# Attention and a quantised convolution block: band statistics behind both halves, and the last block's tail, the count and the scale factors at other places

## The chip, the cores and the metric

The kernel runs on one core of a Trainium2 chip. The metric is the device time of one execution in microseconds (us); the time of a kernel is the median of several runs. A profiled execution gives the trace, in which PE is TensorE's matmul, PEld its weight load, DVE VectorE, ACT ScalarE, POOL GpSimd and SP SyncE, which here only issues DMAs.

## The reference

Two layers on x of 4 x 128 x 64 x 64 in fp32. Cut to what is computed:

```python
# layer 0: group norm, attention with 4 heads of 32 channels over 4096 positions, projection, residual
x_norm = _group_norm(x, norm_w, norm_b)                    # 8 groups
qkv = einsum('oc,bchw->bohw', qkv_w, x_norm) + qkv_b
attn = softmax(einsum('bhid,bhjd->bhij', q, k) * scale)
out = einsum('bhij,bhjd->bhid', attn, v)                   # back to b, c, h, w
x = x + einsum('oc,bchw->bohw', proj_w, out) + proj_b
# layer 1: two 3x3 convolutions with weights quantised to 3 bits, each with batch norm
residual = x
out = relu(batchnorm(conv3x3(x, lsq_quantize(w1, alpha1)), gamma1, beta1))
out = batchnorm(conv3x3(out, lsq_quantize(w2, alpha2)), gamma2, beta2)
return relu(out + residual)
```

## The kernel before

Every engine works through its instructions in the order in which the program issues them; the order is written out by hand, and waits come from the tiles: whoever reads a tile waits for its writer, whoever writes it again waits for its readers. Tiles come from pools with a fixed number of buffers, so a new tile can wait for an old one's last reader. In PSUM there are three buffers of two banks (`pss`, for scores and for convolution sums) and two of one bank (`psa`). In SBUF a ring of nine buffers (`stack_tile`, one free buffer after the other in the order of their release) holds the attention's keys and, later, the bands and their parts.

*Attention.* 32 blocks (4 images, 8 query blocks each), 32 steps of key rows to a block. PE makes scores in groups of three half steps (L442), ACT takes exponentials (L444), PE weighs the values with them (L456) into `acc`, DVE adds the exponentials up (L471), and a few are added by DMA (`rm`, L466). `schedule` hangs other work on the half steps of a block; `ends` are the half steps that close a group of three. There the next image's norm is made: `late[b]` is the list of its steps, of which number 5 (L281, L282: two products for the biases of k and q, tile `gb`) and 6 (L286, their subtraction) stand at the first such slot of one block for each of three images, 7 and 8 (`gw`, `bvn`) at the third.

*The end of a block* is a chain (`finish_parts`): copy `acc` to `av` (ACT), `merge` the two sums (a DMA that adds, `r<-rm`, POOL's queue), `sums` over rows on PE (L488, tile `l`), `spread` the 2048 totals over partitions by DMA (`lq<-ls`), `invert` them on DVE and write them out (`rd<-rq`), adding totals and reciprocals to `worst`; `gather` them with copies by DMA (`rc<-rd`), `weigh` (`av` times `rc`, DVE L520), `project` (PE, tile `po`), `store` (DVE L530 adds bias and residual `x`, POOL's queue writes `y`). For all blocks but the last this chain is hung on the next block. For the last it is woven into the first convolution.

*Convolutions.* The image is cut into 16 bands of 16 rows, each of two halves of 512 positions. A band is loaded (`load_band`, SP's queue; POOL sets its borders, L543 to L549) and split into a high and a low part for exact products. A plain band (0, 1, 5, 8, 11, 15) takes 36 products, 18 to a half (`conv`, L811). The other ten are done two rows at a time (`conv_by_two`, L843) with 24 products: DVE makes sums and differences of rows (`begin`: L578 to L581, ACT copies them, L583), then the low parts (`rest`, L587); from the products the band's rows are put together by `copy` (ACT L853), `inner` (DVE L856, L857) and `outer` (L860, L862), and ACT sums squares (L948). For a plain band DVE takes statistics (`stats`, L904) and ACT copies the sums out (`keep`, L909). `stats` and `keep` read one half each of a tile that holds both; `origin` makes the shift of the squares from band 0's statistics. The split of band m+2 is made while band m's products run, and band m+3 is loaded.

`layer` runs this for a convolution; `first` says what the first one does beside each band. `opening` is the order of its bands 0 and 1, with the last block's chain up to `weigh`; `project` and `store` follow at band 3. At band 5 `count_bad` looks whether any total was out of range: a maximum over `worst` and a comparison on DVE, a product `nbad` of one number on PE in a buffer of `psa`, and a cast to `cnt` (L986 to L991), which every engine reads at the end to choose whether a general version is to run. Also at band 5 the second layer's quantised weights are loaded from `wqd` to `raw_w`, a buffer of the ring, and at band 6 DVE casts them to their own tile. Ahead of the first convolution DVE makes six scale factors of one column each for the batch norms (L870 to L872). `batch_norm` ends each layer.

The second convolution works in the same way (`second`); then the residual, loaded again from `y`, is added, and the output written.

Of the kernel before, what the change touches and what calls it, by code (L numbers as in the profile page):

```python
# [22 lines left out]
P = 128  # L23
# [55 lines left out]
def _fast_body(ctx, tc, x, norm_w, norm_b, qkv_wt, qkv_b, proj_wt, proj_b,  # L79
# [584 lines left out]
    def schedule(n, before):  # L664
        b, qb = blocks[n]
        todo = []
        ends = [p for p in range(2 * NK - 2) if (2 * n * NK + p) % 3 == 2]
        two = b + 1 < B and qb in ((3, 4, 5) if b == 0 else (2, 3))

        def at_half(p, f):  # L670
            todo.append((p, f))

        def add(kt, f):
            todo.append((2 * kt + 1, f))

        def visit(i, first, second, evacuate=None, split=True):
            at_half(ends[i], first)
            e = ends[i + 1 if split else i]  # L680
            at_half(e, second)
            if evacuate:
                at_half(e + 1, evacuate)
            return e

        if before:
            add(1, before["merge"])
            e = visit(5 if two or n == 1 else 6, lambda: before["sums"](0), lambda: before["sums"](1),
                      split=not two and n != 1)
            at_half(e + 2, before["spread"])  # L690
            at_half(e + 8, before["invert"])
            at_half(e + 12, before["residual"])
            at_half(e + 15, before["gather"])
            at_half(ends[18] - 4, before["weigh"])
            at_half(ends[18], before["project"])
            at_half(ends[18] + 2, before["store"])
        if n + 1 < len(blocks):
            add(22 if n == 0 else 14, lambda: load_q(*blocks[n + 1]))
        if n == 0:
            for i, what, j in ((0, "k", 5), (2, "v", 4), (4, "k", 6), (6, "v", 5), (8, "k", 7),  # L700
                               (10, "q", 1), (12, "v", 6), (14, "v", 7)):
                visit(i, *first_chunk(j, what, False), split=False)
                if what == "k":
                    at_half(ends[i] + 5, lambda j=j: load_k(0, j))
        if n == 0:
            for j in (2, 3):
                add(25 + j, lambda j=j: fetch(0, j))
        if n == 1:
            for i, j in zip((1, 3, 8, 10, 12, 14), range(2, NB)):
                if j > 3:  # L710
                    at_half(ends[i - 5], lambda j=j: fetch(0, j))
                visit(i, *project_parts(0, j, lambda j=j: xin[0, j])["q"], split=False)
        qn = qb if b else qb - 1
        if b + 1 < B:
            if qn == 1:
                st = small.tile([P, NB, 6], F32, name=f"st{b + 1}", tag="st")
                for j in range(NB):
                    add(3 * j // 2, lambda j=j: fetch(b + 1, j))
                    add(3 * j // 2 + 3, lambda j=j: nc.vector.bn_stats(st[:, j, :], xin[b + 1, j]))
                late[b] = norm_parts(b + 1, st)  # L720
                add(15, late[b][0])
                for i in (0, 1):
                    at_half(ends[13 + 2 * i], late[b][1 + 2 * i])
                    at_half(ends[13 + 2 * i] + 3, late[b][2 + 2 * i])
            if qn == 2:
                at_half(ends[0], late[b][5])
                at_half(ends[0] + 1, late[b][6])
                at_half(ends[2], late[b][7])
                at_half(ends[2] + 1, late[b][8])
            if b == 0:  # L730
                chunks = {2: (), 3: (0, 1), 4: (2, 3), 5: (4, 5), 6: (6,), 7: (7,)}
            else:
                chunks = {1: (), 2: (0, 1), 3: (2, 3), 4: (4,), 5: (5,), 6: (6,), 7: (7,)}
            for i, j in enumerate(chunks.get(qb, ())):
                p = project_parts(b + 1, j, lambda j=j: xin[b + 1, j])
                if not two:
                    for what, i in dict(k=1, q=10, v=13).items():
                        visit(i, *p[what])
                    continue
                for what, e in (dict(k=3, q=7, v=9) if i == 0 else dict(k=11, q=13, v=15)).items():  # L740
                    visit(e, *p[what], split=False)
                if i == 1:
                    add(8, lambda j=j: fetch(b + 1, j))
            if qn > 0 and qb + 1 in chunks:
                add(22, lambda j=chunks[qb + 1][0]: fetch(b + 1, j))
            if qb == NB - 1:
                for j in range(NB - 1):
                    add(4 * j + 1, lambda j=j: load_kv(b + 1, j))
        if b > 0 and qb == 0:
            add(9, lambda: load_k(b, NB - 1))  # L750
            add(16, lambda: load_v(b, NB - 1))


        if b == B - 1 and qb < NB - 1:
            for kt in (3, 11, 21):
                add(kt, lambda: next(pieces, None))
        elif 0 < b and qb == 0:
            for kt in (3, 12, 17, 22, 26) + ((29,) if b == 1 else ()):
                add(kt, lambda: next(pieces))
        if n == len(blocks) - 1:  # L760
            add(5, lambda: load_band(0, 0))
            add(13, lambda: split_band(0, 0))
            add(17, lambda: load_band(0, 1))
            add(24, lambda: split_band(0, 1))
            add(27, lambda: load_band(0, 2))
        return sorted(todo, key=lambda t: t[0])
# [80 lines left out]
    def rows_of_two(a, c, y, sums):  # L847
# [11 lines left out]
        def outer():  # L859
# [6 lines left out]

    a_q, a_g, a_n = ([small.tile([P, 1], F32, name=f"{n}{i}") for i in range(2)]
                     for n in ("aq", "ag_", "an"))
    for i in range(2):
        nc.vector.tensor_tensor(a_q[i], alpha_s[i], alpha_s[i], ALU.mult)  # L870
        nc.vector.tensor_tensor(a_g[i], alpha_s[i], bn[i][0], ALU.mult)
        nc.vector.tensor_scalar(a_n[i], a_g[i], -1.0, None, ALU.mult)  # L872

    def batch_norm(i, st):

# [121 lines left out]

    def first(m):
        begin = rest = nothing
        if 2 < m < len(bandlist) - 2:  # L1000
            begin, rest = parts_of(0, m + 2, raw[bandlist[m + 2]])

        def later():
            if m == 3:
                last = parts[len(blocks) - 1]
                last["project"]()
                last["store"]()
                att.close()
                pools["low"] = ctx.enter_context(tc.tile_pool(name="low", bufs=1, reuse_waits="tile"))
                cv.extend(pools["low"].tile([P, N], F32, name=f"cv{b}") for b in (2, 3))  # L1010
            if m == 5:
                count_bad()
                raw["w"] = f32(stack_tile("raw_w"))[:, : TAPS * P].rearrange("p (t o) -> p t o", o=P)
                nc.sync.dma_start(out=raw["w"], in_=wqd)
            if m == 6:
                nc.vector.tensor_copy(wq[1], raw["w"])
            if 2 < m < len(bandlist) - 3:
                load_band(*bandlist[m + 3])

        return begin, rest, later  # L1020

    def opening(banks, stats, keep, origin):
        last = parts[len(blocks) - 1]
        last["merge"]()
        e = [conv_tile(0, *bandlist[m]) for m in range(2)]
        conv(ready[0, 0, 0], e[0][:, 0, :], 0, wq[0])
        begin, rest = parts_of(0, 2, raw[bandlist[2]])
        begin()
        load_band(*bandlist[3])
        stats(0, 0, e[0])  # L1030
        keep(0, 0, e[0])
        conv(ready[0, 0, 0], e[0][:, 1, :], 1, wq[0])
        mix_weights(0)
        rest()
        last["residual"]()
        stats(0, 1, e[0])
        keep(0, 1, e[0])
        origin()
        conv(ready[0, 0, 1], e[1][:, 0, :], 0, wq[0])
        last["sums"](0)  # L1040
        last["sums"](1)
        last["spread"]()
        begin, rest = parts_of(0, 3, raw[bandlist[3]])
        begin()
        load_band(*bandlist[4])
        conv(ready[0, 0, 1], e[1][:, 1, :], 1, wq[0])
        stats(1, 0, e[1])
        keep(1, 0, e[1])
        last["invert"]()
        last["gather"]()  # L1050
        rest()
        stats(1, 1, e[1])
        keep(1, 1, e[1])
        done = banks(2)
        conv_by_two(ready[0, 0, 2], *done, 0)
        begin, rest = parts_of(0, 4, raw[bandlist[4]])
        begin()
        last["weigh"]()
        rest()
        load_band(*bandlist[5])  # L1060
        return {0: None, 1: None, 2: done}
# [532 lines left out]
```

## Time and profile before

| what | value |
|---|---|
| time, median of 3 runs | 2502.31 us (2500.63 to 2504.02) |
| profiled execution | 2501.34 us, its span 2499.6 us |
| PE busy | 2452.0 us (98%) |
| DVE busy | 2205.0 us (88%) |
| ACT busy | 2150.3 us (86%) |
| POOL busy | 282.3 us (11%) |
| first product of the first convolution | at 2230.46 us |
| first product of the second convolution | at 2359.34 us |
| end of the last product's line, c_last | DVE reads it at 2469.33 us |

The span runs from the first to the last instruction; the execution's time has 1.7 us around it. The attention takes the first 2230 us, the two convolutions some 240, the end some 30. An engine's busy share over the whole span says little about a stage of 60 us, so for the change the timeline of each engine from 2230 to 2360 us is read. In a timeline a line has its start, its length, the engine, the line of the program, the operation, what it writes and from what, how many instructions are merged, and in brackets how long the engine sat idle before it and who ended that. In a list of waits the numbers are the total, how often, and the longest.

### The profile page before, as it was taken

The page shows a single profiled execution, that of the slowest core. Times are in us where ns is not written, and L with a number is a line of the kernel's source. Part 1 is how long each engine was busy: PE and PEld are TensorE (multiplying, and loading weights), DVE is VectorE, ACT ScalarE, POOL GpSimd, SP SyncE. Part 2 cuts the span into 40 slices and gives each one's busy share as a digit, 9 for nine tenths or more (in the row PEclk, how much of TensorE's full clock was granted, in tenths as well). Part 3 has the DMA queues.
Part 4 walks back from the last instruction along what each step waited for, and adds up shares of the span by engine and source line. Part 5 has one row for each costly group of instructions (what it writes and reads, how often), then busy time and mean ns, then how long its engine had stood idle before and what let it go on. Part 6 is the DMA issues. An engine that isn't in the chain of part 4 may idle for free. (4 is left out here: it accounts for less than half of the span.)

```text
span 2499.6 us, 64813 instructions
## 1 busy us (share of the span) xinstructions
PE 2452.0 (98%) x28468; PEld 1463.4 (59%) x28468; DVE 2205.0 (88%) x1554; ACT 2150.3 (86%) x2347; POOL 282.3 (11%) x464
## 2 busy tenths in 40 slices
PE   9999999999999999999999999999999999999995
PEld 6555555555555555555555555555555555556774
DVE  6899888899988888889988898889999999997787
ACT  5999888999988899999988899999999999964475
POOL 2111111111011111110011111110000000110000
PEclk9999999999999999999999999999999999999998
DMA  6877677688766766788767766788656656665205
GB/s 197 191 183 171 165 176 176 167 202 193 180 154 164 182 163 164 161 204 193 163 149 184 168 157 168 172 203 188 146 130 152 143 132 149 152 139 111 86 1 203
DMA packets 149506, 405.17 MB, mean 162 GB/s; under 512 B 59712, under 2 KB 60480, under 8 KB 120544
## 3 DMA queue, kind: packets, MB, share of 16 engines
q0 software_dynamic: 45984, 281.44, 49.2%
q1 hardware_dynamic: 101360, 113.87, 17.4%
q8 instruction: 225, 3.69, 0.6%
q10 hardware_dynamic: 1872, 5.64, 0.6%
q14 instruction: 65, 0.53, 0.1%
HBM read 107.75 MB, written 56.43 MB: 66 GB/s over the span
## 5 line engine op out<-in xcount | busy, mean ns | idle before, releaser
L444 ACT ACTIVATE p<-s 128x1024 f32<-128x1024 f32 x2048 | 1951.3, 1033 | 197.9 <-PE s L442 152.6
L471 DVE TENSOR_TENSOR r<-r,p 128x2048 f32<-128x2048 f32 x768 | 1758.1, 2289 | 63.9 <-ACT p L444 13.2
L442 PE MATMUL s<-q,k 64*128 64x512 f32 x8192 | 1137.3, 409 | 1.2 <-ACT p L444 1.2
L456 PE MATMUL acc<-p,v 128*32 128x256 f32 x16384 | 1025.9, 383 | 0.0
L442 PEld LDWEIGHTS s<-q,k 64*128 64x128 f32 x8192 | 717.1, 185 | 406.3 <-issue 163.5
L456 PEld LDWEIGHTS acc<-p,v 128*32 128x32 f32 x16384 | 464.0, 109 | 481.8 <-issue 247.8
L466 POOL DMA_DIRECT2D rm<-p x160 | 139.1, 870 | 796.7 <-ACT p L444 618.3
L352 DVE SCALAR_TENSOR_TENSOR kst<-pk,b,kst 128x512 fp32r<-128x512 f32 x32 | 24.0, 751 | 82.7 <-PE s L442 62.3
L469 DVE TENSOR_TENSOR r<-p,p 128x2048 f32<-128x2048 f32 x32 | 73.2, 2288 | 11.7 <-ACT p L444 11.6
L948 ACT ACTIVATE uo<-cv,shift 128x1024 fp32r<-128x1024 f32 x20 | 23.1, 1153 | 61.0 <-DVE cv L862 57.3
L352 DVE SCALAR_TENSOR_TENSOR qst<-pq,b,qst 128x512 fp32r<-128x512 f32 x32 | 24.0, 750 | 58.2 <-PE s L442 47.3
L356 POOL DMA_DIRECT2D qd<-qst x31 | 23.6, 760 | 266.4 <-DVE qst L352 222.8
L811 PE MATMUL c<-hi,wq 128*128 128x512 f32 x180 | 48.4, 415 | 5.3 <-ACT cv L909 4.0
L492 POOL DMA_DIRECT2D r<-rm x32 | 27.0, 844 | 225.5 <-DMA rm<-p 93.8
L811 PE MATMUL c<-lo,wq 128*128 128x512 f32 x180 | 46.6, 404 | 0.0
L811 PEld LDWEIGHTS c<-hi,wq 128*128 128x128 f32 x180 | 34.8, 195 | 15.6 <-ACT cv L909 4.5
L356 POOL DMA_DIRECT2D kd<-kst x27 | 20.0, 741 | 175.7 <-DVE kst L352 167.2
L811 PEld LDWEIGHTS c<-lo,wq 128*128 128x128 f32 x180 | 34.4, 191 | 9.2
L317 PE MATMUL po<-av,wp 128*32 128x512 f32 x256 | 33.4, 593 | 4.6 <-DVE cv L860 3.2
L488 PE MATMUL l<-r,ones 128*32 128x256 f32 x512 | 37.7, 379 | 0.0
L464 POOL DMA_DIRECT2D rm<-p x32 | 17.9, 558 | 174.1 <-DMA r<-rm 82.3
L351 ACT ACTIVATE kst<-pk,b 128x512 fp32r<-128x512 f32 x32 | 22.3, 700 | 17.7 <-PE pk L317 17.6
(252 smaller groups left out, 1142.9 us busy)
## 6 DMA issues: line engine op xcount, KB each, us to landing
rm<-p POOLq DMA_DIRECT2D x192, 1024.0 KB, 7.9
r<-rm POOLq DMA_DIRECT2D x32, 1024.0 KB, 7.6
q<-qd SPq DMA_DIRECT2D x248, 128.0 KB
x<-in_x_dram SPq DMA_DIRECT2D x86, 256.0 KB
k<-kd SPq DMA_DIRECT2D x124, 128.0 KB
qd<-qst POOLq DMA_DIRECT2D x31, 512.0 KB, 5.7
kd<-kst POOLq DMA_DIRECT2D x27, 512.0 KB, 4.6
rc<-rd SPq DMA_DIRECT2D x32, 256.0 KB
```

Of the source, the lines that this page charges most:

```text
L317: nc.tensor.matmul(out[cs, :], w[:, cs], x, start=True, stop=True)
L352: nc.vector.scalar_tensor_tensor(lo, ps[what], bias, t[:, 0, :], ALU.add, ALU.subtract)
L356: (nc.sync if start else nc.gpsimd).dma_start(out=dst[b, j].rearrange("s p n -> p s n"), in_=t)
L442: nc.tensor.matmul(s[:, i, :], k[r, half, c0 : c0 + P], q[r, half, part, :], start=(part == 0), stop=(part == 1))
L444: nc.scalar.activation(pts[step][:, 2 * half : 2 * half + 2, :], s, AF.Exp, scale=SCALE)
L456: nc.tensor.matmul(acc[n][h * D : (h + 1) * D, cs], v[:, kt % KB, h * D : (h + 1) * D], pt[:, h, cs], start=(kt == 0 and half == 0), stop= ...
L466: nc.gpsimd.dma_start(out=msum[n], in_=pt, accum_op=ALU.add)
L469: nc.vector.tensor_tensor(rsum[n], pts[step - 1], pt, ALU.add)
L471: nc.vector.tensor_tensor(rsum[n], rsum[n], pt, ALU.add)
L488: nc.tensor.matmul(t["l"][h * D : (h + 1) * D, cs], ones, r[:, h, cs], start=first, stop=end)
L492: nc.gpsimd.dma_start(out=rsum[n], in_=msum[n], accum_op=ALU.add)
L811: nc.tensor.matmul(ps.rearrange("p (r w) -> p r w", w=W), w[:, tap, :], part[:, r0 + kh : r0 + kh + RB, kw : kw + W], start=(n == 0), stop ...
```

## The change

Six things are moved or left out:

- In `schedule` the norm's bias products and their subtraction stand at the second slot of the block instead of the first.
- In `opening` band 0's `stats` and `keep` of both halves are issued after the second half's products, the mixing of the weights, the low parts of band 2 and the load of the residual. For band 1 both pairs follow the low parts of band 3, `invert` and `gather`.
- `weigh` of the last block is issued at band 3, ahead of that band's `begin`, where before it stood in the opening between `begin` and `rest` of band 4's parts.
- `count_bad` goes from band 5 to band 14.
- The second layer's weights are loaded by DMA to their tile, without `raw_w` and the cast.
- The six scale factors are made at band 11.

```diff
             if qn == 2:
-                at_half(ends[0], late[b][5])
-                at_half(ends[0] + 1, late[b][6])
+                at_half(ends[1], late[b][5])
+                at_half(ends[1] + 1, late[b][6])
                 at_half(ends[2], late[b][7])
                 at_half(ends[2] + 1, late[b][8])
...
-    for i in range(2):
-        nc.vector.tensor_tensor(a_q[i], alpha_s[i], alpha_s[i], ALU.mult)
-        nc.vector.tensor_tensor(a_g[i], alpha_s[i], bn[i][0], ALU.mult)
-        nc.vector.tensor_scalar(a_n[i], a_g[i], -1.0, None, ALU.mult)
+
+    def scales():
+        for i in range(2):
+            nc.vector.tensor_tensor(a_q[i], alpha_s[i], alpha_s[i], ALU.mult)
+            nc.vector.tensor_tensor(a_g[i], alpha_s[i], bn[i][0], ALU.mult)
+            nc.vector.tensor_scalar(a_n[i], a_g[i], -1.0, None, ALU.mult)
...
     def first(m):
         begin = rest = nothing
+        last = parts[len(blocks) - 1]
         if 2 < m < len(bandlist) - 2:
             begin, rest = parts_of(0, m + 2, raw[bandlist[m + 2]])
+        if m == 3:
+            mix = begin
+
+            def begin():
+                last["weigh"]()
+                mix()
 
         def later():
             if m == 3:
-                last = parts[len(blocks) - 1]
                 last["project"]()
                 last["store"]()
...
             if m == 5:
+                nc.sync.dma_start(out=f32(wq[1]), in_=wqd)
+            if m == 11:
+                scales()
+            if m == 14:
                 count_bad()
-                raw["w"] = f32(stack_tile("raw_w"))[:, : TAPS * P].rearrange("p (t o) -> p t o", o=P)
-                nc.sync.dma_start(out=raw["w"], in_=wqd)
-            if m == 6:
-                nc.vector.tensor_copy(wq[1], raw["w"])
...
         load_band(*bandlist[3])
-        stats(0, 0, e[0])
-        keep(0, 0, e[0])
         conv(ready[0, 0, 0], e[0][:, 1, :], 1, wq[0])
         mix_weights(0)
         rest()
         last["residual"]()
-        stats(0, 1, e[0])
-        keep(0, 1, e[0])
+        for j in range(2):
+            stats(0, j, e[0])
+            keep(0, j, e[0])
         origin()
...
         conv(ready[0, 0, 1], e[1][:, 1, :], 1, wq[0])
-        stats(1, 0, e[1])
-        keep(1, 0, e[1])
+        rest()
         last["invert"]()
         last["gather"]()
-        rest()
-        stats(1, 1, e[1])
-        keep(1, 1, e[1])
+        for j in range(2):
+            stats(1, j, e[1])
+            keep(1, j, e[1])
...
         begin, rest = parts_of(0, 4, raw[bandlist[4]])
         begin()
-        last["weigh"]()
         rest()
```

## The prediction

> **What bounds the kernel now.** I read the page first (TensorE, PE, busy 98% of the span), then the list of waits with PE as the one that waits, from 2228 us on, where most of the change lies (columns: who waited for whom, total us, times, longest):
>
> ```profile
> PE c L811 <- ACT cv L909: 4.0, 1, 4.0
> PE po L317 <- DVE cv L860: 3.2, 1, 3.2
> PE nbad L990 <- DVE bad L988: 2.3, 1, 2.3
> PE c L811 <- ACT hi L1081: 1.2, 1, 1.2
> ```
>
> PE sets the end, and in two convolution layers it stops for under 12 us. The first three stops are at edited places. PE's timeline:
>
> ```profile
> 2232.70 2.32 PE L811 MATMUL c<-lo,wq 128*128 128x512 f32 x9
> 2239.03 4.21 PE L811 MATMUL c<-hi,wq 128*128 128x512 f32 x9 [4.02 <-ACT cv L909]
> 2243.03 2.74 PE L811 MATMUL c<-lo,wq 128*128 128x512 f32 x9
> 2245.61 2.30 PE L811 MATMUL c<-hi,wq 128*128 128x512 f32 x9
> 2247.75 2.31 PE L811 MATMUL c<-lo,wq 128*128 128x512 f32 x9
> 2249.99 1.07 PE L488 MATMUL l<-r,ones 128*32 128x256 f32 x16
> ...
> 2270.22 1.06 PE L317 MATMUL po<-av,wp 128*32 128x512 f32 x8 [3.23 <-DVE cv L860]
> 2271.22 1.61 PE L843 MATMUL c<-ui,wmix 128*128 128x512 f32 x3
> ...
> 2289.61 0.19 PE L990 MATMUL nbad<-ones,bad 128*1 128x1 f32 x2 [2.27 <-DVE bad L988]
> 2289.73 0.98 PE L843 MATMUL c<-ui,wmix 128*128 128x512 f32 x3
> ```
>
> After two of the stops the same products run slowly: 18 products of half a band take 6.58 us from 2239.03, 4.38 from 2245.61. The windows (length; then PE, PEld, DVE, ACT, POOL busy; granted clock; DMA) show why:
>
> ```profile
> 2239.00:2243.00 4.00, 3.97 (x9) 3.14 (x10) 3.19 (x4) 0.00 (x0) 0.00 (x0) 0.50 0.49 98
> 2270.20:2273.00 2.80, 2.78 (x12) 1.62 (x13) 0.96 (x3) 2.13 (x4) 0.00 (x0) 0.69 0.34 54
> 2310.00:2330.00 20.00, 20.00 (x86) 15.77 (x85) 17.46 (x26) 9.80 (x13) 0.41 (x5) 1.00 0.57 151
> ```
>
> VectorE (DVE) in the same stretch, and then at the end of the first layer:
>
> ```profile
> 2265.21 0.69 DVE L520 TENSOR_TENSOR av<-av,rc 128x512 f32<-128x512 f32 x1 [3.16 <-DMA rc<-rd]
> ...
> 2347.06 0.69 DVE L856 TENSOR_TENSOR cv<-cv,c 128x512 f32<-128x512 f32 x1 [1.84 <-ACT cv L853]
> 2347.78 0.69 DVE L857 TENSOR_TENSOR cv<-c,cv 128x512 f32<-128x512 f32 x1
> 2348.39 0.68 DVE L860 SCALAR_TENSOR_TENSOR cv<-cv,c_2z 128x512 f32<-128x512 f32 x1
> ```
>
> The weighing (L520) stands on DVE for its DMA, and the sums that free a PSUM bank for the projection (L860) stand behind it. The one wait in the attention that an edit touches:
>
> ```profile
> 728.84 0.38 PE L281 MATMUL gb<-gc,wqkv 128*128 128x1 f32 x2 [1.11 <-ACT av L481]
> ```
>
> **What the Trainium skill says.** "TensorE: Matmul & The Clock Gate", Part 1: after about 3.4 us idle PE runs at half clock, for a window of that length. The trace agrees: 0.50 after the 4.02 us stop, 0.69 after 3.23, 1.00 (window from 2289.70) after 2.27. "PSUM — Partial Sum Buffer", PSUM bank collisions: engines must be kept apart by bank. The wait at 2239.03 is coarser: half 1 has a bank of its own but the same tile, whose half 0 was still to be read. The same page calls the DVE and ACT queues strict FIFO (Engine vs sequencer instructions), as L860 behind L520 shows.
>
> **The change part by part.**
>
> *1, band 0's statistics behind both halves.* Nothing reads the tile before half 1's products are issued, so the 4.02 us go, and the slow clock, 6.58 - 4.38 = 2.20. DVE does the weights' mixing and the two low parts first. I re-ran the order with the trace's durations: DVE starts at 2234.18 (the six scale factors, 2234.18 to 2234.84, are gone from here), is done with `rest` at 2240.9, PE with half 1 at 2239.4. Statistics and copies alternate (0.7 us of DVE idle each time, as at 2291.30), to 2243.6. The totals on PE start at about 2243.7 and need the merge DMA, issued 2234.56 and landing 6.9 us later, 2241.5: 2.2 us to spare.
>
> *2, band 1 and the reciprocals.* Low parts of band 3 and reciprocals come before the statistics, which wait for PE till 2249.2. The spread DMA goes at 2245.5 instead of 2251.74, and band 4's load behind it on SP's queue at 2246.1; DVE inverts at 2248.8. Before, `rc` landed 8.9 us after the reciprocal (2256.21 to some 2265.1), so now at about 2257.8. Band 4's load moved its bytes in 4.5 us before: it lands at 2250.7, and DVE wants it at 2251.2.
>
> *3, weighing behind band 2's sums.* DVE ends L862 of band 2 at 2258.55 and weighs to 2259.2, while PE ends band 3 at 2260.8. The bank is free and `av` ready: the 3.23 us stop goes, and its slow clock (band 4: 2271.22 to 2278.58 is 7.36, warm 5.72: 1.64). The store (L530) ends at 2263.6, before PE wants its bank for band 4 (2265.9). What is late next: `rc`, with 1.4 us to spare at PE.
>
> *4, the count moved from band 5 to band 14.* The 2.27 us stop goes, and with it nbad's own 0.12. But it comes back at the new place. Count and sums are queued on DVE behind `inner` of band 14, which ends at 2348.39 (old time), PE is through with that band at 2347.09. From the start of `big` to nbad took 0.40 (2289.21 to 2289.61): 2348.79, so PE stands 1.70 + 0.12 = 1.82 us ahead of the last band. Behind `cnt` on DVE waits only `outer` of 14, done well before the last band's statistics. The stop is too short for the slow clock. Bounds: 0.1 if DVE is early, 3 if later by a few instructions.
>
> *5, second layer's weights straight into their tile.* The 0.75 us cast at 2296.14 and a buffer of the ring go; SP waited 7.9 us for that buffer. SP also waited 9.9 us for `cnt` between the loads of bands 8 and 9; it can now wait only behind the last band's load, before residual loads that have the whole second layer. PE never waited for these loads: 0. Scale factors at band 11: 0.66 us on DVE, which sat idle 0.53 there before L904; 0.
>
> *6, the norm's bias products from the first to the second slot*, in three blocks. Only at 728.84 did PE wait, for a copy queued on ACT behind three exponentials; a group later the copy is done. Gain 1.1; bounds 0 and 1.2. DVE's b is still ahead of the next slot.
>
> *Sum.* From 2230.46 to band 6 (2289.73) PE takes 59.27 us. Warm and unbroken, from the same rows: 3 x 4.38 (three halves) + 1.00 (totals) + 4.40 + 5.73 + 5.72 (bands 2, 3) + 1.00 (projection) + 5.72 + 8.60 (bands 4, 5) = 45.31. Gain 13.96, of it 9.52 waits, 3.84 slow clock, the rest pipeline ends. DVE keeps ahead: band 6's low parts are ready at 2271.0, PE gets there at 2275.9. From band 6 on PE has no wait before, so the gain is carried. 13.96 - 1.82 + 1.1 = 13.2. The profiled execution took 2501.34 (span 2499.6 and 1.7 around it): 2488.1. Its distance to the median 2502.31 is 1.0, so 2489.1.
>
> **The rivals.**
> *A, the reciprocals come late.* The way out and back (rd, then rc) now runs beside band 4's load and with bands 5 and 6 close behind. For: rd is issued with 1.6 us of that load left. Against: bands 5 and 6 followed it as closely before. If rc lands as late as before, 2265.1, PE stands from 2260.8 to 2265.9 and then pays about 2 us of slow clock: 13.2 - 5.1 - 2 = 6.1, 2496. Chance 0.08.
> *B, no change.* The stop at nbad grows over the clock's window (3.5 us and 2 more) and rc is as late as in A: 6.1 - 3.7 = 2.4, 2500. DVE's idle at 2341.29 and 2347.06 speaks against a long queue there. Chance 0.05.
> *C, slower.* The same way of the reciprocals, much longer: with weighing at the head of DVE's queue, band 3's sums, the store, its memsets on POOL and every later band stand behind it. It costs PE one for one from 2260.2 on. Gain is used up when rc lands at about 2272, and 2510 needs it at 2280, some 30 us after its issue; it took 7.3 before, and in block 30 at most 17.5 (2203.85 to the weighing at 2221.32) beside the attention's traffic. Chance 0.06.
>
> **How the numbers follow.** Forecast 0.81, A 0.08, B 0.05, C 0.06. The likeliest gives 2489.1. Its own range: the stop at nbad from 0.1 to 3 (-1.7, +1.2), part 6 up to +1.1, a first part of A up to +3: 2486.5 to 2494. Some of the forecast's chance lies outside that, so the range is taken on to A's time: 2486.5 to 2496.5, with B and C left out. 0.2% is 5 us, about what a measurement of this kernel tells from none: faster 0.88 (forecast and most of A), same 0.06, slower 0.06.
>
> **What would show it.** Right: PE's list of waits loses L811 <- ACT cv and po, has nbad at about 1.7 us just ahead of c_last, none at gb; clock 1.00 from the first band on; band 6 starts some 45 us after the first product. Wrong: a new wait of PE on av or l, DVE standing at L520 for rc, or a stop at nbad over 3.4 us with a clock below 1 behind it.

## The result, and the profile after

| | before | after |
|---|---|---|
| median | 2502.57 us (2500.63 to 2505.54, 6 runs) | 2490.87 us (2490.34 to 2492.34, 6 runs) |
| profiled execution's span | 2499.6 us | 2489.0 us |
| first product of the first convolution | 2230.46 us | 2231.53 us |
| from there to the first product of the second ("the length") | 128.88 us | 116.86 us |
| from there to the end of the span | 140.29 us | 140.61 us |

The ratio is 0.9953, with a 95% interval of 0.994 to 0.9966: faster by 11.7 us by the medians. The prediction was 2489.1, in a range of 2486.5 to 2496.5. Most figures below are lengths, since the attention ahead varies by a few us from one profile to the next and the first convolution's stretch hardly does (116.84 in a second profile of the same kernel).

PE's list of waits in the profile after, from 2228 us on, first (total, times, longest), then lines of PE's timeline (start, length, engine, line, operation, idle before):

```profile
PE nbad L992 <- DVE bad L990: 1.5, 1, 1.5
PE c L811 <- POOL t L544: 1.2, 1, 1.2
PE c L843 <- ACT cv L911: 0.7, 1, 0.7
```

```profile
2233.77 2.32 PE L811 MATMUL c<-lo,wq 128*128 128x512 f32 x9
2235.93 2.30 PE L811 MATMUL c<-hi,wq 128*128 128x512 f32 x9
2238.06 2.31 PE L811 MATMUL c<-lo,wq 128*128 128x512 f32 x9
...
2261.52 1.06 PE L317 MATMUL po<-av,wp 128*32 128x512 f32 x8
2262.52 0.99 PE L843 MATMUL c<-ui,wmix 128*128 128x512 f32 x3
...
2276.94 0.88 PE L843 MATMUL c<-ui,wmix 128*128 128x512 f32 x3
...
2335.98 0.19 PE L992 MATMUL nbad<-ones,bad 128*1 128x1 f32 x2 [1.51 <-DVE bad L990]
2336.10 2.41 PE L811 MATMUL c_last<-hi,wq 128*128 128x512 f32 x9
```

The 4.0 us at the second half of band 0 and the 3.2 us at the projection are gone; no bracket stands at 2235.93 or 2261.52. The 2.27 us at the count have become 1.51 us, now ahead of the last band. Band 6 starts 45.41 us after the first product (2276.94 - 2231.53), where it started after 59.27. The clock (the last three figures of a window are clock, DMA share and GB/s) is full where it was at half, and also behind the stop of 1.51 us; over the whole stretch from 2231.50 to 2276.90 it is 1.00:

```profile
2236.00:2246.00 10.00, 10.00 (x55) 7.29 (x54) 9.21 (x16) 3.60 (x5) 1.15 (x9) 1.00 0.52 105
2336.10:2340.00 3.90, 3.90 (x18) 3.12 (x17) 2.63 (x13) 1.24 (x2) 0.00 (x0) 1.00 0.00 0
```

DVE's timeline shows the weighing without a wait, and at the end of the layer what the count's product waits for:

```profile
2259.49 0.69 DVE L520 TENSOR_TENSOR av<-av,rc 128x512 f32<-128x512 f32 x1
2261.41 0.69 DVE L856 TENSOR_TENSOR cv<-cv,c 128x512 f32<-128x512 f32 x1 [1.24 <-ACT cv L853]
...
2334.25 0.69 DVE L856 TENSOR_TENSOR cv<-cv,c 128x512 f32<-128x512 f32 x1 [1.84 <-ACT cv L853]
2334.97 0.69 DVE L857 TENSOR_TENSOR cv<-c,cv 128x512 f32<-128x512 f32 x1
2335.58 0.16 DVE L988 TENSOR_REDUCE big<-worst 128x1 f32<-128x16 f32 x1
2335.77 0.15 DVE L990 TENSOR_SCALAR bad<-big 128x1 f32<-128x1 f32 x1
```

The maximum and the comparison stand behind band 14's sums, which wait for an ACT copy; PE is through with that band at 2334.5 and gets its operand at 2336.

### The profile page after: what moved, and what is told of

It reads as the page before. It is cut to its first block, busy times and chain, and to the rows that moved or that the text cites. A ratio compares the mean times of both kernels' runs of the same rounds, so it can differ in the third digit from the quotient of the medians.

```text
span 2489.0 us, 64807 instructions
## 1 busy us (share of the span) xinstructions
PE 2449.8 (98%) x28468; PEld 1457.1 (59%) x28468; DVE 2204.9 (89%) x1553; ACT 2150.2 (86%) x2347; POOL 283.3 (11%) x464
## 5 line engine op out<-in xcount | busy, mean ns | idle before, releaser
L471 DVE TENSOR_TENSOR r<-r,p 128x2048 f32<-128x2048 f32 x768 | 1758.3, 2289 | 63.6 <-ACT p L444 13.2
L531 POOL DMA_DIRECT2D y<-x x32 | 21.7, 679 | 126.8 <-DVE x L530 126.8
```

Source lines behind the costliest of these rows:

```text
L471: nc.vector.tensor_tensor(rsum[n], rsum[n], pt, ALU.add)
```

## The experiments

Two theories were to be told apart. Mine: every stop of PE in this stretch counts one for one, and a long one is paid again in slow products; the change moves the work so that the stops go. The rival: DVE is the limit, and what helped was work taken off it (the cast, the scale factors, the count), or a queue freed on SP. Times are medians against runs of the kernel before on the same chip; stops and lengths are from each run's profile.

**b_part1: only band 0's statistics moved.** To the kernel before:

```diff
-        stats(0, 0, e[0])
-        keep(0, 0, e[0])
         conv(ready[0, 0, 0], e[0][:, 1, :], 1, wq[0])
...
-        stats(0, 1, e[0])
-        keep(0, 1, e[0])
+        for j in range(2):
+            stats(0, j, e[0])
+            keep(0, j, e[0])
```

> The kernel before with band 0's statistics and copies behind both halves, all else as before. First layer's length (first product of the first convolution to first product of the second) was 128.9 us before, 116.9 after. Theory (each stop of PE counts one for one, and a stop of 3.2 us or more also costs some 2 us of half clock): the 4.0 us stop and 2.2 us of slow clock go, the stop at the projection stays at about 3.1 us since the reciprocals come 6 us earlier but the weighing still stands ahead of band 4's low parts: 122.5 us. Rival (DVE is the true limit, relieved by the scale factors, the cast and the count): under 2 us gained, 127 or more.

2496.52 us, ratio 0.9971 (0.996 to 0.9981); length 124.09. PE's timeline and two windows:

```profile
2265.26 1.06 PE L317 MATMUL po<-av,wp 128*32 128x512 f32 x8 [2.26 <-DVE cv L860]
2284.65 0.19 PE L990 MATMUL nbad<-ones,bad 128*1 128x1 f32 x2 [3.27 <-DVE bad L988]
```

```profile
2284.70:2288.00 3.30, 3.30 (x10) 2.59 (x11) 1.45 (x3) 1.17 (x2) 0.00 (x0) 0.50 0.17 38
2265.00:2268.00 3.00, 2.74 (x15) 1.58 (x16) 1.16 (x5) 2.10 (x4) 0.00 (x0) 1.00 0.40 62
```

The stop at the projection is shorter than I had it (2.26 for 3.1), as the weighing got `rc` 8.0 us after the reciprocal began instead of 9.0, and it costs no slow clock. But the stop at the count grew from 2.27 to 3.27: counted from the first product, PE reached it 8.4 us sooner than before and DVE only 7.4. The clock was at half behind it: band 6 takes 8.48 us (2284.77 to 2293.25) against 5.72 warm. So part 1 alone gained 4.8 us of length where I expected 6.4. The rival's "under 2" is out: nothing was taken off DVE here.

**b_filler: PE kept busy during the stop.** To the kernel before, products that nobody reads:

```diff
         keep(0, 0, e[0])
+        keep_warm(14)
         conv(ready[0, 0, 0], e[0][:, 1, :], 1, wq[0])
```

> The kernel before with 28 products of 128 columns put on PE between the two halves of band 0; they compute nothing that is used. Theory (half clock because PE was idle): half 1 still starts at about 8.6 us after the first product, its clock is 1.00, its 18 products take 4.4 instead of 6.6 us, and the layer is about 2 us shorter than before though PE does more: 126.9 us. Rival (the products were slow for the memory's or the merge DMA's sake): 6.6 us still, 128.9.

2502.99 us, ratio 0.9997 (0.9989 to 1.0006); length 127.64. PE's timeline, DVE's line for the weighing, and windows on the second half of band 0 and behind the projection:

```profile
2237.03 3.29 PE L310 MATMUL idle<-gavg 128*128 128x128 f32 x28
2241.25 2.42 PE L811 MATMUL c<-hi,wq 128*128 128x512 f32 x9 [0.94 <-ACT cv L909]
2243.51 2.31 PE L811 MATMUL c<-lo,wq 128*128 128x512 f32 x9
...
2271.13 1.94 PE L317 MATMUL po<-av,wp 128*32 128x512 f32 x8 [4.10 <-DVE cv L860]
```

```profile
2266.12 0.69 DVE L520 TENSOR_TENSOR av<-av,rc 128x512 f32<-128x512 f32 x1 [4.03 <-DMA rc<-rd]
```

```profile
2241.00:2245.00 4.00, 3.75 (x16) 2.98 (x17) 3.38 (x5) 0.20 (x1) 0.24 (x3) 1.00 0.49 98
2271.00:2275.00 4.00, 3.87 (x13) 1.83 (x14) 2.13 (x7) 2.80 (x4) 0.00 (x0) 0.50 0.32 51
```

Half 1's 18 products take 4.41 us (2241.25 to 2245.66) instead of 6.58, at full clock, with as much DMA traffic as in the window from 2239.00 in the profile before (98 GB/s, 0.49 of the DMA engines). So the slow products came from PE's own idleness, not from the memory. The length is 1.24 us shorter, not 2, and the medians show no difference: the stop at the projection is 0.9 us longer and the slow products behind it cost 1.2 more, while the stop at the count is 1.15 shorter (1.12 for 2.27). The reciprocal began sooner too (23.64 us after the first product, for 25.75 before), but DVE began the weighing 9.9 us after it (2256.25 to 2266.12) and not 9.0.

**a_between: part 1 undone.** To the kernel after:

```diff
+        stats(0, 0, e[0])
+        keep(0, 0, e[0])
         conv(ready[0, 0, 0], e[0][:, 1, :], 1, wq[0])
...
-        for j in range(2):
-            stats(0, j, e[0])
-            keep(0, j, e[0])
+        stats(0, 1, e[0])
+        keep(0, 1, e[0])
```

> The kernel after with band 0's first statistics and copy back between its halves. Theory: PE stops there for 3.4 us (0.66 less than before, since the scale factors are no longer ahead of DVE's work), with 0 to 2.2 us of slow clock behind it as the stop falls beside the clock's window: length 120.3 to 122.5 us against 116.9. Rival (other work takes the time anyway): under 118.

2495.71 us, ratio 0.9971 (0.9958 to 0.9983); length 121.99, or 5.1 more than after. PE's timeline and its window:

```profile
2238.29 3.74 PE L811 MATMUL c<-hi,wq 128*128 128x512 f32 x9 [3.36 <-ACT cv L911]
2241.82 2.52 PE L811 MATMUL c<-lo,wq 128*128 128x512 f32 x9
```

```profile
2238.30:2241.70 3.40, 3.40 (x9) 2.74 (x10) 3.15 (x4) 0.00 (x0) 0.00 (x0) 0.59 0.76 154
```

The stop is 3.36 us as expected, and the products behind it take 5.89 us (2238.29 to 2244.18), 1.5 more than warm. Nothing later made up for it.

**a_weigh_early: the weighing back in the opening.** To the kernel after:

```diff
-        if m == 3:
-            mix = begin
-
-            def begin():
-                last["weigh"]()
-                mix()
...
         begin()
+        last["weigh"]()
         rest()
         load_band(*bandlist[5])
```

> The kernel after with the weighing back between begin and rest of band 4's parts. Theory: rc lands some 8.9 us after the reciprocal, DVE stands at the weighing for about 4 us, the bank for the projection comes 2 us late and PE stops there for 2.1 us without slow clock: length 119.0 us against 116.9. Rival A (rc lands much later than I took it, but hidden behind other work): over 121. Rival (the weighing's place is worth nothing once the reciprocals come early): 117.

2497.13 us, ratio 0.9973 (0.9962 to 0.9984); length 121.76, so 4.9 more than after and not 2.1. DVE's lines for the weighing and for the first sums of bands 3 and 14, then PE's lines and two windows:

```profile
2257.25 0.69 DVE L520 TENSOR_TENSOR av<-av,rc 128x512 f32<-128x512 f32 x1 [3.14 <-DMA rc<-rd]
...
2264.65 0.69 DVE L856 TENSOR_TENSOR cv<-cv,c 128x512 f32<-128x512 f32 x1 [1.84 <-ACT cv L853]
...
2337.11 0.69 DVE L856 TENSOR_TENSOR cv<-cv,c 128x512 f32<-128x512 f32 x1 [1.84 <-ACT cv L853]
```

```profile
2262.26 1.06 PE L317 MATMUL po<-av,wp 128*32 128x512 f32 x8 [1.19 <-DVE cv L860]
2268.09 0.99 PE L843 MATMUL c_0y<-uo,wq 128*128 128x512 f32 x3 [0.28 <-DVE x L530]
...
2338.84 0.19 PE L992 MATMUL nbad<-ones,bad 128*1 128x1 f32 x2 [2.97 <-DVE bad L990]
2338.96 3.70 PE L811 MATMUL c_last<-hi,wq 128*128 128x512 f32 x9
2342.46 2.57 PE L811 MATMUL c_last<-lo,wq 128*128 128x512 f32 x9
```

```profile
2337.00:2340.00 3.00, 1.16 (x6) 0.92 (x7) 2.54 (x8) 0.07 (x1) 0.00 (x0) 0.94 0.00 0
2340.00:2344.00 4.00, 4.00 (x13) 3.15 (x12) 1.70 (x10) 1.24 (x2) 0.00 (x0) 0.62 0.00 0
```

The weighing began as soon as `rc` was there, 8.1 us after its reciprocal (2249.14), where before it took 9.0 (2256.21 to 2265.21). The stop at the projection is smaller than expected (1.19), as rc was earlier than I took it. The rest is far away: the stop at the count has doubled to 2.97 us, and the last band's first half takes 5.90 us instead of 4.4 (clock 0.62 from 2340 to 2344). Counted from the first product, DVE begins the sums of band 3 3.8 us later than in the kernel after and those of band 14 still 3.4 us later, while PE is 1.9 us late by then. So a DVE that is late at band 3 is still late at band 14. This gave the next question.

**a_count5: the count back at band 5.** To the kernel after:

```diff
             if m == 5:
+                count_bad()
                 nc.sync.dma_start(out=f32(wq[1]), in_=wqd)
...
-            if m == 14:
-                count_bad()
```

> The kernel after with the count of bad sums back at band 5. Theory (the count's product stops PE wherever DVE runs behind it, so the move itself gains next to nothing): PE stops at nbad for about 1.5 us beside band 5 instead of 1.5 us ahead of the last band: length 116.9 us as after. Rival (the move saves the 2.27 us that the trace of before shows): 118 to 119.

2490.24 us, ratio 0.995 (0.9934 to 0.9965); length 116.66. The stop stands at band 5 again:

```profile
2277.45 0.19 PE L992 MATMUL nbad<-ones,bad 128*1 128x1 f32 x2 [1.31 <-DVE bad L990]
```

So with the other parts in place, moving the whole count gains nothing; it is 0.2 us the other way.

**a_split: the comparison early, the product late.** To the kernel after:

```diff
-    def count_bad():
+    bad = small.tile([P, 1], F32, name="bad")
+
+    def mark_bad():
         big = small.tile([P, 1], F32, name="big")
         nc.vector.tensor_reduce(big, worst, AX.X, ALU.max)
-        bad = small.tile([P, 1], F32, name="bad")
         nc.vector.tensor_scalar(bad, big, LIMIT, None, ALU.is_gt)
+
+    def count_bad():
         nbad = psa.tile([P, FB], F32, name="nbad", tag="a")
...
+            if m == 8:
+                mark_bad()
             if m == 11:
                 scales()
```

> The kernel after with the count in two: maximum and comparison on DVE at band 8, the product and the cast at band 14 as after. Theory: the operand lies ready six bands earlier, the stop of 1.5 us at nbad goes and nothing takes its place: length 115.3 us against 116.9. Rival (the last band waits for something else at that point, a bank of PSUM or the sums of band 14): 116.9.

2489.16 us, ratio 0.9941 (0.9927 to 0.9954); length 115.29. PE's timeline has no bracket at nbad:

```profile
2334.59 0.87 PE L843 MATMUL c_2z<-lo,wq 128*128 128x512 f32 x3
2335.39 0.19 PE L994 MATMUL nbad<-ones,bad 128*1 128x1 f32 x2
2335.51 2.42 PE L811 MATMUL c_last<-hi,wq 128*128 128x512 f32 x9
```

**a_weigh_split: both edits at once**, the diffs of a_weigh_early and a_split.

> The kernel after with both edits: the weighing back between begin and rest of band 4's parts, and the count in two, its comparison at band 8. Theory (a DVE late at band 3 stays late for eleven bands, and only the count's product lets PE feel it): the stops of 1.3 and 0.3 us at band 3 and 4 stay, the stop of 3.0 us at nbad and its slow clock go: length 115.3 + 1.6 = 116.9 us, 4.9 less than with the weighing early alone. Rival (the lateness reaches PE in any case, at a bank of PSUM or a low part): 119 or more.

2491.11 us, ratio 0.9948 (0.9935 to 0.9962); length 117.11. PE's list of waits:

```profile
PE po L317 <- DVE cv L860: 1.1, 1, 1.1
PE c L843 <- ACT cv L911: 0.7, 1, 0.7
PE c_0y L843 <- DVE x L530: 0.3, 1, 0.3
```

The stops at bands 3 and 4 are as in a_weigh_early, the one at nbad is gone with its slow clock. So the weighing's place is worth 1.8 us by itself (117.11 - 115.29), and 4.9 with an operand for PE that DVE makes just in time eleven bands later (121.76 - 116.86).

**after_again and a_split_again: the two side by side.**

> The kernel after, for comparison on the same chip: length 116.9 us; time about 2491 us.

> The count in two once more, beside the kernel after on the same chip: length 115.3 us, no stop at nbad; time 1.6 us under that of the kernel after, which the medians may not resolve.

2491.64 us (0.9951, 0.9937 to 0.9964) and 2489.55 us (0.9942, 0.9929 to 0.9956); lengths 116.84 and 115.28. The length repeats to 0.02 us; the intervals of the two ratios overlap, so the split's 1.6 us are shown by the profiles and not by the medians alone.

**a_gb0: the norm's bias products back at the first slot.** To the kernel after:

```diff
-                at_half(ends[1], late[b][5])
-                at_half(ends[1] + 1, late[b][6])
+                at_half(ends[0], late[b][5])
+                at_half(ends[0] + 1, late[b][6])
```

> The kernel after with the norm's bias products back at the first slot. Theory: PE waits 1.1 us for the copy of acc at the start of block 10 again, so that block ends 1.1 us later against the blocks before it; the first layer's length stays 116.9. In the whole time 1.1 us is hardly to be seen beside what the attention varies by itself. Rival (the wait is made up for later in the block): no difference by the block's end.

2493.05 us, ratio 0.9959 (0.9944 to 0.9974); length 116.87. PE's line in this run, then in the profile after:

```profile
729.68 0.38 PE L281 MATMUL gb<-gc,wqkv 128*128 128x1 f32 x2 [1.11 <-ACT av L481]
```

```profile
731.57 0.38 PE L281 MATMUL gb<-gc,wqkv 128*128 128x1 f32 x2
```

The wait is back. From the copy of `acc` of block 9 to that of block 10 it takes 72.53 us in all four profiles with the old place, and 71.37 to 71.47 in the nine with the new one. So some 1.1 us are won at that place; the medians do not resolve it.

**a_ring: the weights through the ring and the scale factors at their old place.** To the kernel after:

```diff
+    scales()
+
     def batch_norm(i, st):
...
-                nc.sync.dma_start(out=f32(wq[1]), in_=wqd)
-            if m == 11:
-                scales()
+                raw["w"] = f32(stack_tile("raw_w"))[:, : TAPS * P].rearrange("p (t o) -> p t o", o=P)
+                nc.sync.dma_start(out=raw["w"], in_=wqd)
+            if m == 6:
+                nc.vector.tensor_copy(wq[1], raw["w"])
```

> The kernel after with the second layer's weights again loaded into the ring at band 5 and cast by DVE at band 6, and the six scale factors again ahead of the first convolution. Theory: DVE has 1.4 us more to do where it has slack and SP no wait that PE sees: length 116.9 us, within 0.3. Rival (DVE is the limit, and taking work off it is where the gain came from): 118.3 or more.

2491.48 us, ratio 0.9952 (0.9937 to 0.9967); length 116.89. Putting 1.4 us of work back on DVE changed nothing in the first convolution; with b_part1 and a_count5 this ends the rival. The stretch from the second convolution to the end is 0.3 us shorter (140.32 against 140.61); whether the ring or the scale factors do that wasn't tried apart, and b_part1, which has both as before, stands at 140.54.

## Why the prediction was right, point by point

*Parts 1 to 3, PE's 13.96 us up to band 6.* 45.41 us were measured for 45.31. The order re-run by hand held at each point that can be read, counted from the first product: `rest` done at 10.53 us (10.44 foretold), totals on PE at 13.06 (13.24), spread at 14.81 (15.04), the weighing at 27.96 (28.09), the store's sum done at 33.18 (33.14), band 6's low parts at 40.45 (40.54). It held because each engine keeps its order and its steps take as long as before (L587 1.25 us in both profiles). PE's end of band 3, put at 2260.8, was a slip: the prediction's own rows give 2260.45, and that came (29.99 us after the first product). a_between, b_part1 and a_weigh_early show that the places are what counts. The earlier spread, though, is the work of part 1 and not of part 2: in b_part1 it is issued 14.80 us after the first product, for 21.28 before and 14.81 after. Part 2 then brings the reciprocal from 19.28 to 18.13 us. Part 2 was not undone by itself, so what its order is worth otherwise is not shown.

*The slow clock.* That it follows from PE's idleness, as the Trainium skill has it ("TensorE: Matmul & The Clock Gate", Part 1), is shown by b_filler. The page's figure of about 3.4 us is not borne out as the limit: the clock already fell at recorded stops of 3.23 us (before) and 2.97 us (a_weigh_early). The first of these stood in the prediction as agreeing with the page, which it does not quite.

*Rivals A and C, the reciprocals.* In the five profiles in which DVE stood at the weighing, it began 8.0 to 9.9 us after the reciprocal. With the 8.1 of a_weigh_early, rc had an estimated 1.7 us in hand when DVE came to it in the kernel after (26.24 against 27.96 us after the first product), and the wait never arose. With the 9.9 of b_filler nothing would have been left for DVE; by the same estimate the weighing would have ended at 28.7 us, still ahead of PE at 29.99.

*Part 4, the count.* The stop came back at the place foretold, 1.51 + 0.12 us for 1.70 + 0.12. The bound of 3 us was priced without slow clock, and there the prediction was wrong: at 2.97 us a_weigh_early paid 1.5 us more. That the whole move gains next to nothing was not said so plainly: I booked 2.27 as gone and 1.82 as new. a_count5 shows that once the other stops go, the old place would have cost 1.3. The total is right all the same, since it was taken from one whole order to the other; only the share booked for the move was wrong.

*Part 5* was booked at nothing. In the first convolution it is. Over the rest to the end the kernel after is 0.3 us slower, and a_ring wins that back; but as b_part1 is nearly as slow there (140.54) without part 5, the 0.3 is not shown to be theirs.

*Part 6.* 1.1 us, as foretold.

*The sum.* Foretold were 13.2 us. The profiles give 12.02 (length) and 1.07 (blocks 9 and 10, where the copy was 0.88 us later at block 9 and 0.19 earlier at block 10), less 0.3 at the end: 12.8. The span shows 10.6, because the rest of the attention took 2.1 us more in the profile after. That is not the change: the first product of the first convolution came at 2230.46, 2232.61, 2232.94 and 2233.82 us in the four profiles with the old order of the attention, and at 2230.38 to 2232.60 in the nine with the new one; on the mean the new ones are 1.0 us earlier, about what part 6 should give. The profile that I summed from was the quickest of its four. What remains between 11.7 by the medians and 12.8 lies within the runs' own spread.

## What to carry to other kernels

Where one engine sets the end, list its stops in the stretch, price each as its length plus the slow products behind it, and re-run the order of every queue by hand with the trace's durations; that gave the times on the engines listed above to 0.25 us, while the way through the two DMAs was off by about 1 us. A stop that goes uncovers the next lateness: an engine with little slack stays late for many steps, and the operand that it makes just in time for the first engine is where that is paid, so make such operands early and only use them late. Here moving a whole step with its product did not remove the wait; splitting it did.

## What the runs showed of the hardware

Stops and the clock: PE ran at full clock after stops of 1.51, 2.26 and 2.27 us, and slowed after 2.97, 3.23, 3.27, 3.36, 4.02 and 4.10 us. The price was not in step with the stop: 1.5 us after 2.97 and 3.36, 1.6 after 3.23, 2.76 after 3.27, 2.2 after 4.02, 2.8 after 4.10. Why stops of nearly one length differ so is not shown, and none between 2.27 and 2.97 was seen here. So a stop of 3.0 us can already cost half as much again, and one of 3.3 nearly twice its length.

The whole stretch of 117 us repeats to 0.02 us between two profiles of one kernel, while the attention ahead of it varies by more than 3 us (first product at 2230.46 to 2233.82 with one order of the attention). What it varies by was not looked into.

DVE's lateness was hardly made up in this stretch: in a_weigh_early it fell from 3.8 us at band 3 to 3.4 at band 14.
